# Queries of five row tiles made in natural order at the end of part one; their first 512 rows open part two

## The chip, the cores and the metric

The kernel runs on one core of one Trainium2 chip. Its engines work side by side and each takes its own instructions in order: TensorE (PE in the profile; its weight loads are PEld), VectorE (DVE), ScalarE (ACT), GpSimd (POOL) and SyncE (SP), which issues plain DMAs. GpSimd also issues the indirect DMAs, here called gathers. The metric is the device time of one execution in microseconds; lower is better. The time before is 1229.44 us, the median of three runs (1226.88, 1229.44 and 1234.75).

## The reference

The input x has N = 3327 rows of D = 1024 floats, and adj is a 3327 x 3327 matrix of 0 and 1, symmetric, with ones on the diagonal and few others: a row has from a handful to some tens of neighbours. What is computed is one graph attention layer behind a layer norm:

```python
h = jnp.maximum(_layernorm(x, axis=-1), 0.0)
f = h @ Wf + bf
g = h @ Wg + bg
e = jax.nn.relu(f @ g.T)
scores = jnp.where(adj > 0, e, NEG)
attention = jax.nn.softmax(scores, axis=1)
out = x + attention @ (h @ W + bW)
```

The three weight matrices are 1024 x 1024. A row's softmax runs only over its neighbours.

## The kernel before

The kernel never forms the 3327 x 3327 scores. Since f . g of two rows is h A h with A = Wf Wg^T, it makes A once, then a query q = h A (plus the bias terms) for each row, and takes the dot product of that query with the h row of each neighbour. Rows go in tiles of 128, so there are 26 tiles, the last with 127 rows. A dense path stands behind a flag for inputs with rows of too many neighbours; it does not run here.

**Part one** (some 240 us) goes through the 26 natural tiles. For each it loads the adjacency rows, counts degrees on ScalarE (`degrees`, L697), multiplies the 0/1 row with column numbers on GpSimd (`keys`, L704), takes the largest eight of each of 16 segments on VectorE (`segments`, L767) and builds a list of up to 24 neighbours in `pay` (`listed`). It also loads x, makes layer norm and relu (`measured`, `rooted`, `inverted`, `scaled`), and stores h in DRAM (`hd`). Beside this TensorE transposes Wg and Wf in blocks (`transposed`, `factor`, L821), and makes the products of A in thirds of 342 columns (`product`, L837); a ninth product row holds the bias term `vb`. ScalarE copies each result out of PSUM, in the order in which `empty` finds it. The loop over i issues the degrees and keys of tile i + 2 and the segments and list of tile i. A dictionary `plan` spreads the product steps over the iterations.

A counting sort orders all rows by degree. `one_hot` marks each row's degree among 48 bins; `before` and `after` (L798, L801) accumulate counts in one PSUM tile `pre`; `placed` (L806, the "hit") reads a row's place. At the end 26 small matmuls (L1078) turn places into the order of rows, `perm` (L1092). Part one then gathers the h rows of the first two sorted tiles, transposes them, and makes their q (L1108) on TensorE.

**Part two** (some 970 us) goes through the sorted tiles. The capacity of a tile, `CAPS`, is the largest number of neighbours of its rows; `ORDER` is the sequence in which the tiles are done. For each tile GpSimd gathers the lists (from `pd`), the tile's own h rows (H), and, one gather per neighbour place, 128 h rows (G, all L639). TensorE transposes H and makes q in thirds (L1246). VectorE takes a dot product of each gathered tile with q (L1259, whole result into `junk`, sum into `sc`), masks, and finds the maximum; ScalarE takes the exponentials. The weighted sum of gathered rows is split: `SHARE` says how many rows of a tile's last chunk ScalarE scales and TensorE adds up in PSUM by a transposing matmul (L1295, L1299); VectorE adds the rest (L1312). TensorE then multiplies with W (L1327), and the rows are added to x and scattered to the output.

The order of the instructions of part two is worked out when the program is built: `steps_of` lists all steps with costs and dependences, `planned` runs a list schedule forward and backward 30 times with noise and keeps the best order, and each engine's queue has that order. `FREE_AT` gives the time at which the planner takes each engine as free. The plan only sets orders; what an instruction waits for at run time are its data and buffers. `ROWS` = 26 buffers hold gathered rows; two `junk` tiles take turns.

## Time and profile before

| | us |
|---|---|
| runs | 1226.88, 1229.44, 1234.75 |
| the profiled execution | 1226.98 |
| its span, first to last instruction | 1225.2 |
| VectorE busy | 1116.6 (91%) |
| TensorE busy | 1098.0 (90%) |
| GpSimd busy | 942.2 (77%) |
| ScalarE busy | 602.7 (49%) |

A share of the whole span hides the stages, so the views by stretch of time and the timeline are of more use here. In a line of the timeline the first two numbers are the start and the length in us; then come engine, source line, operation, output and inputs, shapes and count. What stands in brackets at the end is the time for which the engine had been idle, and what ended that.

### The profile page before, as it was taken

Reading aid. Unit: us, or ns where it says so; the run is one execution under the profiler, and the core shown is the slowest. Engines: PE = TensorE matmul, PEld = TensorE weight load, DVE = VectorE, ACT = ScalarE, POOL = GpSimd, SP = SyncE. Lnnn points to the kernel's source line nnn. Section 1 sums busy time; section 2 is a strip of 40 time slices with the busy share of each in tenths; the row PEclk is TensorE's granted clock in tenths of the full one; section 3 lists DMA queues with packets and bytes.
Section 4 is the critical chain, followed back from the end, with each engine's and each line's share of the span. In section 5 each row is a group of like instructions: output and inputs, shape, how many; then the busy total and the mean of one; then the engine's idle time right before and its main releaser. Section 6 shows DMA issues by size and latency. Waiting matters only on the chain. (4 is left out here: it accounts for less than half of the span.)

```text
span 1225.2 us, 14006 instructions
## 1 busy us (share of the span) xinstructions
PE 1098.0 (90%) x4508; PEld 697.0 (57%) x4508; DVE 1116.6 (91%) x2191; ACT 602.7 (49%) x924; POOL 942.2 (77%) x677
## 2 busy tenths in 40 slices
PE   2799990799939899899999999999899999999997
PEld 2566660466628466556665666655465656555553
DVE  5999998659898999999999999898999999999983
ACT  6899887325617355436543365443332434333351
POOL 8999997277677787878888878777787888877841
PEclk9899995799979999999999999999899999999999
DMA  9999999689888999989999998888988989998962
GB/s 369 420 398 396 397 356 338 199 318 339 280 259 278 333 308 316 347 273 326 305 331 316 321 310 299 289 285 296 314 285 284 312 275 320 295 315 258 326 183 54
DMA packets 101913, 374.43 MB, mean 306 GB/s; under 512 B 14859, under 2 KB 18602, under 8 KB 98631
## 3 DMA queue, kind: packets, MB, share of 16 engines
q0 software_dynamic: 79584, 286.77, 69.9%
q1 hardware_dynamic: 22246, 86.68, 18.7%
q8 instruction: 37, 0.61, 0.2%
q14 instruction: 46, 0.38, 0.1%
HBM read 344.11 MB, written 29.30 MB: 305 GB/s over the span
## 5 line engine op out<-in xcount | busy, mean ns | idle before, releaser
L639 POOL DMA_INDIRECT G<-hd,ps x454 | 569.2, 1254 | 152.6 <-issue 96.9
L1259 DVE CUSTOM_DVE_ANT_0 junk<-G,q 128x1024 bf16<-128x1024 f32 x468 | 564.2, 1225 | 35.5 <-DMA G<-hd,ps 21.1
L1327 PE MATMUL p_o<-W_sb,yT 128*128 128x512 f32 x832 | 365.7, 593 | 3.7 <-ACT yT L1323 3.7
L1312 DVE SCALAR_TENSOR_TENSOR G<-G,sc 128x1024 f32<-128x1024 f32 (+1 forms) x281 | 354.8, 1263 | 6.1 <-ACT G L1284 5.4
L1246 PE MATMUL p_q<-A_sb,hT 128*128 128x342 f32 x1152 | 350.3, 455 | 8.7 <-ACT p_q L1255 7.3
L1246 PEld LDWEIGHTS p_q<-A_sb,hT 128*128 128x128 f32 x1152 | 214.4, 191 | 117.0 <-issue 10.0
L1327 PEld LDWEIGHTS p_o<-W_sb,yT 128*128 128x128 f32 x832 | 155.1, 189 | 187.9 <-issue 177.1
L1299 PE MATMUL p_y<-ident,G 128*128 128x128 f32 x1552 | 189.3, 276 | 15.1 <-DVE G L1312 8.3
L1299 PEld LDWEIGHTS p_y<-ident,G 128*128 128x128 f32 x1552 | 174.9, 142 | 43.1 <-ACT G L1295 13.5
L704 POOL TENSOR_TENSOR r<-r,iotaj 128x1664 f32<-128x1664 f32 (+3 forms) x50 | 184.0, 3750 | 3.4 <-ACT r L697 3.4
L1295 ACT ACTIVATE G<-G,sc 128x1024 f32<-128x1024 f32 x168 | 179.1, 1137 | 0.1
L837 PE MATMUL ps_A<-WgT,WfT 128*128 128x342 f32 x432 | 129.7, 458 | 2.4 <-ACT WfT L832 2.4
L767 DVE MAX8 cand<-r 128x8 f32<-128x208 f32 (+2 forms) x416 | 118.9, 360 | 4.2 <-POOL r L704 3.6
L1338 ACT ACTIVATE xp<-p_o,rs 128x512 f32<-128x512 f32 x50 | 34.2, 686 | 174.3 <-PE p_o L1327 131.2
L837 PEld LDWEIGHTS ps_A<-WgT,WfT 128*128 128x128 f32 x432 | 81.3, 192 | 42.3 <-ACT WfT L832 2.5
L697 ACT ACTIVATE r<-r 128x3327 f32<-128x3327 int32 (+3 forms) x27 | 77.3, 2864 | 12.1 <-DMA r<-in_adj_dram 12.1
L1252 ACT COPY q<-p_q 128x342 f32<-128x342 f32 x72 | 31.5, 441 | 103.7 <-PE p_q L1246 74.3
L639 POOL DMA_INDIRECT xp<-in_x_dram,perm x25 | 49.4, 1974 | 19.9 <-ACT xp L1338 13.2
L1280 ACT ACTIVATE sc<-sc,nm 128x10 f32<-128x10 f32 (+10 forms) x36 | 10.9, 303 | 106.2 <-DVE nm L1270 86.6
L1242 ACT COPY hT<-p_t 128x512 f32<-128x512 f32 x48 | 27.3, 585 | 72.3 <-PE p_t L1239 42.9
L1323 ACT COPY yT<-p_y 128x512 f32<-128x512 f32 x52 | 30.0, 586 | 59.9 <-PE p_y L1299 59.9
L1345 POOL DMA_INDIRECT out_dram<-xp,perm x25 | 31.3, 1252 | 35.8 <-DMA xp<-in_x_dram,perm 30.9
(147 smaller groups left out, 724.6 us busy)
## 6 DMA issues: line engine op xcount, KB each, us to landing
r<-in_adj_dram SPq DMA_DIRECT2D x24, 1663.5 KB, 13.1
xt<-in_x_dram SPq DMA_DIRECT2D x22, 512.0 KB, 13.6
hd<-xt SPq DMA_DIRECT2D x22, 512.0 KB, 10.5
G<-hd,ps POOLq DMA_INDIRECT x454, 6.1
A_sb<-in_L_gnn_Wg_dram SPq DMA_DIRECT2D x8, 512.0 KB, 17.1
A_sb<-in_L_gnn_Wf_dram SPq DMA_DIRECT2D x8, 512.0 KB, 12.0
W_sb<-in_L_gnn_W_dram SPq DMA_DIRECT2D x8, 512.0 KB, 6.4
cd<-cand SPq DMA_DIRECT2D x25, 64.0 KB, 12.6
```

Source lines behind the costliest of these rows:

```text
L639: return nc.gpsimd.indirect_dma_start(out=to, out_offset=None, in_=table, in_offset=bass.IndirectOffsetOnAxis(ap=idx, axis=0), **kw,)
L697: nc.scalar.activation(r[:n, b:e], a[:n, b:e], AF.Sign, accum_out=to)
L704: eng.tensor_mul(r[:n, b:e], r[:n, b:e], iotaj[:n, b:e])
L767: nc.vector.max(cands[t][:n, s * 8 : s * 8 + 8], r[:n, s * SW : min(N, (s + 1) * SW)])
L837: nc.tensor.matmul(ps[:, :QB], WfTs[c][:, k, :], WgT[:, k, o : o + QB], start=(k == 0), stop=(k == KD - 1))
L1246: nc.tensor.matmul(ps_q[(3 * t + i) % 2][:, :QB], hT[:, k, :], A_sb[:, k, i * QB : (i + 1) * QB], start=False, stop=(k == KD - 1), skip_gr ...
L1259: nc.vector.tensor_tensor_reduce(junks[k % 2], row(t, k), q[:, :D], 1.0, 0.0, op0=ALU.mult, op1=ALU.add, accum_out=scs[t % 3][:, k : k + 1],)
L1295: nc.scalar.activation(g, g, AF.Copy, scale=scs[t % 3][:, k : k + 1])
L1299: nc.tensor.matmul(ps_y[g][:, c, :], of[:, (4 * g + c) * P : (4 * g + c + 1) * P], ident, is_transpose=True, start=((t, g) not in begun an ...
L1312: nc.vector.scalar_tensor_tensor(y, row_k, scs[t % 3][:, k : k + 1], y, op0=ALU.mult, op1=ALU.add)
L1327: nc.tensor.matmul(ps_o[o], yT[:, k, :], W_sb[:, k, o * CB : (o + 1) * CB], start=False, stop=(k == KD - 1), skip_group_check=True,)
L1338: nc.scalar.activation(to, ps_o[o], AF.Copy, scale=rss[t % 3])
```

## The change

1. At the end of part one the five natural tiles 9, 11, 13, 15 and 17 (`AHEAD`) get their q while their h still lies on the chip: `turn` transposes a tile, `fill` puts the bias into a PSUM bank, `third` multiplies, `stored` copies, and `store_q` writes the tile's q to DRAM (`qd`). These 15 thirds follow the products of A in the same plan (`BEGIN`, `SECOND`, `PERIOD`); the last seven run after the loop, in `go`.
2. Of these 640 rows the 512 of lowest degree among them form the first four tiles of part two (`EARLY`), with capacities 21, 18, 16 and 14, done in the order 14, 16, 18, 21. `several` and `ahead_ranks` rank them among themselves. Their lists are stored on their own (`pd1`, `store_ahead`), and `own` holds their places in `qd` and `pd1`. In part two the H step of these tiles gathers q itself; there is no transposition and no product for them. The other rows are sorted as before into 22 tiles.
3. The sort of the last four natural tiles is done in one go (`pre4`, `less`, `least`) in place of one `before`, `placed`, `after` each.
4. The bias row of the product goes: `bias` multiplies `WgT` with the bias as one column, 9 groups of 8 matmuls, and the result goes through DRAM (`vd`) into `vb`. Wf's first block is loaded earlier, and the three products of the first block are made in iterations 0 to 2.
5. Part one no longer gathers h and makes q for two sorted tiles. W's loads are spread later.
6. G's buffers are one column wider; there is one `junk` tile in place of two, and `masks` and `scs` are narrower.
7. `CAPS`, `ORDER`, `SHARE` and `FREE_AT` are new, and the plan of part two is made anew. The capacities add up to 472 (468 before) and the shares to 184 (168 before).

The core of the diff:

```diff
-CAPS = [37, 25, 23, 22, 21, 21, 20, 20, 19, 19, 18, 18, 17, 17, 17, 16, 16, 15, 15, 15, 14, 14, 13, 13, 12, 11]
-ORDER = [24, 15, *range(15), *range(16, 24), 25]
-SHARE = [9, 11, 18, 12, 10, 9, 10, 8, 7, 7, 8, 8, 5, 8, 4, 4, 4, 4, 3, 3, 3, 2, 3, 0, 5, 3]
+CAPS = [37, 25, 23, 22, 21, 21, 20, 19, 19, 18, 18, 17, 17, 16, 16, 15, 15, 14, 14, 13, 12, 11, 21, 18, 16, 14]
+AHEAD = [9, 11, 13, 15, 17]
+EARLY = len(AHEAD) - 1
+ORDER = [25, 24, 23, 22, *range(22)]
+SHARE = [10, 13, 13, 11, 18, 15, 13, 8, 10, 7, 5, 9, 6, 8, 4, 4, 8, 3, 0, 5, 2, 3, 1, 4, 0, 4]
+BEGIN, SECOND, PERIOD = 40.0, 38.0, 7.5
...
-FREE_AT = {"POOL": 247.6, "PE": 268.5, "ACT": 268.4, "DVE": 246.0, "DMA": 247.0}
+PINS = {("H", EARLY): 0.0, ("H", EARLY + 1): 1.0}
+FREE_AT = {"POOL": 222.0, "PE": 228.0, "ACT": 228.0, "DVE": 237.0, "DMA": 222.0}
...
+        def several(to, ts, start=False):
+            n = len(ts)
+            for j, t in enumerate(ts):
+                count(to[:, j, :], tri, oh[:, t, :], start=start and not j)
+                count(
+                    to[:, j + 1 : n + 1, :], every, oh[:, t, None, :].to_broadcast([P, n - j, NBIN])
+                )
...
+        def bias(c):
+            m = P if c < KD else QW - D
+            for k in range(KD):
+                nc.tensor.matmul(
+                    pv[:m, c : c + 1], WgT[:, k, c * P : c * P + m], bfT[:, k : k + 1], start=(c == k == 0),
+                    stop=(k == KD - 1), skip_group_check=True,
+                )
...
+        def turn(t):
+            hTs[t] = wT.tile([P, KD, P], FP, name="WfT")
+            transposed(hTs[t], xs[t])
+
+        def fill(t, i):
+            banks[t, i] = p_mm.tile([P, CB], FP, name="ps_A")
+            nc.scalar.copy(banks[t, i][:, :QB], vb[:, i * QB : (i + 1) * QB])
+
+        def stored(t, i):
+            nc.scalar.copy(qn[t][:, i * QB : (i + 1) * QB], banks[t, i][:, :QB])
+            if i == 2:
+                q_stores.append(t)
...
+        def store_q():
+            while q_stores:
+                t = q_stores.pop(0)
+                j = AHEAD.index(t)
+                nc.sync.dma_start(qd[j * P : (j + 1) * P, :], qn[t][:, : D + 1])
+
+        def third(t, i):
+            if not i:
+                qn[t] = qpool.tile([P, QW], FP, name="q")
+            for k in range(KD):
+                nc.tensor.matmul(
+                    banks[t, i][:, :QB], hTs[t][:, k, :], A_sb[:, k, i * QB : (i + 1) * QB], start=False, stop=(k == KD - 1),
+                    skip_group_check=True,
+                )
+            emptied1.append(lambda: stored(t, i))
...
+            def turned_g(cs):
+                for c in cs:
+                    if c:
+                        transposed(WgT[:, :, c * P : (c + 1) * P], A_sb[:, c, :D])
+                    empty()
+                    bias(c)
             degrees(0, HALVES)
             keys(0, nc.vector)
+            empty()
+            bias(0)
             degrees(1)
             keys(1, nc.gpsimd)
...
+            turned_g((1, 2))
+            load_w(Wf, 1)
+            load_adj(4)
+            factor(0)
+            empty()
...
             for i in range(NT - 3):
                 degrees(i + 2)
                 keys(i + 2, nc.gpsimd)
...
+                if i < 2:
+                    product(0, i * QB)
+                    turned_g(((3, 4, 5), (6, 7))[i])
+                if i == 1:
+                    biases()
+                    factor(1)
...
-        junks = tiles("junk", 2, [P, D], BF)
+        junk = tiles("junk", 1, [P, D], BF)[0]
...
         def L(t):
-            gather(pis[t % 3], pd[:, :], perm[:, ORDER[t] : ORDER[t] + 1])
+            gather(pis[t % 3], pd1[:, :] if t < EARLY else pd[:, :], near(t))
 
         def H(t):
-            gather(G[buf["H", t]], hd[:, :], perm[:, ORDER[t] : ORDER[t] + 1])
+            to = G[buf["H", t]]
+            gather(to if t < EARLY else to[:, :D], qd[:, :] if t < EARLY else hd[:, :], near(t))
```

After the loop, `go` runs one remaining third at a time: five of them stand in TensorE's queue ahead of the matmuls that find the order of rows, two behind.

369 lines of the change are left out of this document (229 added, 140 removed).

## Prediction

> **What bounds the kernel now.** I read the table of busy time by stretch first, then the timeline where part one hands over to part two, then the timeline of the first 60 us. The columns of the table are the stretch, its length, the busy time of TensorE, of its weight loads, of VectorE, ScalarE and GpSimd (instructions in brackets), the granted clock, the DMA share and GB/s.
>
> ```profile
> span 1225.2 us, 14006 instructions
> ```
> ```profile
> 60.00:80.00 20.00, 20.00 (x80) 13.32 (x80) 19.52 (x81) 19.70 (x31) 20.00 (x7) 1.00 1.03 402
> ```
> ```profile
> 400.00:1000.00 600.00, 570.13 (x2387) 360.60 (x2388) 582.75 (x881) 265.92 (x420) 472.31 (x366) 0.99 0.91 308
> ```
>
> From 60 to 80 us four engines are busy 97% or more, so part one has no idle engine to put work on once it runs. From 400 to 1000 us VectorE is busy 97% and TensorE 95%: part two is paid in VectorE time. The joint between them:
>
> ```profile
> 220.82 0.18 DVE L1092 TENSOR_SCALAR perm<-tens 128x26 int32<-128x26 f32 x1
> ```
> ```profile
> 227.37 1.11 POOL L639 DMA_INDIRECT xt<-hd,perm  x1 [21.33 <-DVE cand L780]
> ...
> 238.72 0.95 POOL L639 DMA_INDIRECT ps<-pd,perm  x1 [8.97 <-DMA pd<-pay]
> ...
> 243.11 0.94 POOL L639 DMA_INDIRECT G<-hd,ps  x1 [0.94 <-DVE mask L1234]
> ```
> ```profile
> 252.56 1.23 DVE L1259 CUSTOM_DVE_ANT_0 junk<-G,q 128x1024 bf16<-128x1024 f32 x1 [9.77 <-ACT q L1128]
> ...
> 266.00 0.15 DVE L1361 CAST flag<-p_y 1x1 int32<-1x1 f32 x1 [5.33 <-PE p_y L1192]
> ```
> ```profile
> 1192.20 10.62 DVE L1312 SCALAR_TENSOR_TENSOR G<-G,sc 128x512 f32<-128x512 f32 x14 [1.02 <-ACT G L1284]
> ```
>
> The order is known at 221.0, the first list gather starts at 238.72, the first row gather at 243.11, the first dot at 252.56 after a wait for q; a second wait of 5.33 follows before tile 1. VectorE then works to 1202.8, and 22.4 us of tail end the span. The last tile has 11 rows of capacity in both orders, so I leave the tail.
>
> **Part two, counted.** Capacities sum to 468 before and 472 after, so four more dots. SHARE sums to 168 and 184, so the weighted additions on VectorE (all rows but row 0 and those of SHARE) fall from 274 to 262.
>
> ```profile
> 253.71 1.22 DVE L1259 CUSTOM_DVE_ANT_0 junk<-G,q 128x1024 bf16<-128x1024 f32 x1
> ...
> 254.86 1.22 DVE L1259 CUSTOM_DVE_ANT_0 junk<-G,q 128x1024 bf16<-128x1024 f32 x1
> ...
> 309.18 1.28 DVE L1312 SCALAR_TENSOR_TENSOR G<-G,sc 128x1024 f32<-128x1024 f32 x1
> 310.38 1.22 DVE L1259 CUSTOM_DVE_ANT_0 junk<-G,q 128x1024 bf16<-128x1024 f32 x1
> ...
> 1188.87 1.22 DVE L1259 CUSTOM_DVE_ANT_0 junk<-G,q 128x1024 bf16<-128x1024 f32 x1
> ```
>
> A dot takes 1.15 (start to start), an addition 1.20: 4 x 1.15 - 12 x 1.20 = -9.8 us. The gap before tile 1 goes, as four tiles no longer need TensorE: -5.3. TensorE loses two tiles of q and gains 16 rows of 8 transposes, a net relief, so VectorE stays the bound.
>
> **One junk tile instead of two.** Consecutive dots now write the same tile. In the trace they overlap: 1.15 apart, 1.22 long, 161 such pairs, of which the first and the last stand above. What a wait inside VectorE costs is seen at the end of part one:
>
> ```profile
> 235.05 0.18 DVE L1150 TENSOR_REDUCE bads<-ne 128x1 f32<-128x26 f32 x1
> ...
> 235.26 0.18 DVE L1151 TENSOR_SCALAR ne<-pay 128x26 f32<-128x26 f32 x1
> ...
> 235.48 0.18 DVE L1152 TENSOR_REDUCE bads<-ne 128x1 f32<-128x26 f32 x1
> 235.58 0.85 DVE L1153 TENSOR_TENSOR r<-r,caps 128x676 bf16<-128x676 bf16 x1
> ```
>
> L1153 shares nothing with L1152 and starts 0.10 after it; L1151 only overwrites what L1150 reads and starts 0.21 after it, 0.03 past its end. A dot held that way would start at 1.22 + 0.03 = 1.25, 0.10 to 0.11 later. Twelve additions fewer and four dots more make some 177 pairs: 19.5 us at most, none if a plain overwrite is not held. Early on gathers rather than VectorE should set the pace, and behind a late row a hold costs nothing, so I take half: +10. The Trainium skill (VectorE: DVE Perf Modes, The DRAIN you can't avoid) has it that the next operation cannot begin until the pipe is empty, so that a semaphore adds nothing; by that the term is 0 and the sum 10 lower. The 0.07 overlap of the dots speaks against it.
>
> **Part one's front.** The change multiplies the bias as 9 groups of 16 small records (bias), puts three products ahead of iteration 3, and takes out the three wide products of the bias row. All sits between the transposes of Wg, and each block's copies on ScalarE stand in its queue ahead of the next degrees (L697), for which GpSimd's key multiply (L704) waits.
>
> ```profile
> 12.85 2.98 ACT L697 ACTIVATE r<-r 128x3327 f32<-128x3327 int32 x1 [3.50 <-DMA r<-in_adj_dram]
> ...
> 35.80 2.98 ACT L697 ACTIVATE r<-r 128x3327 f32<-128x3327 int32 x1
> ```
> ```profile
> 16.00 22.07 POOL L704 TENSOR_TENSOR r<-r,iotaj 128x1664 f32<-128x1664 f32 x6 [2.55 <-ACT r L697]
> 38.94 25.80 POOL L704 TENSOR_TENSOR r<-r,iotaj 128x1664 f32<-128x1664 f32 x7 [0.86 <-ACT r L697]
> ```
> ```profile
> 14.30 1.94 PE L821 MATMUL ps_tr<-ident,A_sb 128*128 128x128 f32 x8 [14.30 <-DMA A_sb<-in_L_gnn_Wg_dram]
> ...
> 45.87 6.77 PE L837 MATMUL ps_A<-WgT,WfT 128*128 128x342 f32 x16 [2.35 <-ACT WfT L832]
> 52.48 1.04 PE L821 MATMUL ps_tr<-ident,A_sb 128*128 128x128 f32 x8
> ...
> 53.41 9.45 PE L837 MATMUL ps_A<-WgT,WfT 128*128 128x342 f32 x32
> ```
> ```profile
> 160.01 0.18 PE L801 MATMUL pre<-oh,low 128*128 128x48 bf16 x1
> 160.04 0.18 PE L798 MATMUL pre<-oh,tri 128*128 128x48 bf16 x1
> ```
> ```profile
> L837 PEld LDWEIGHTS ps_A<-WgT,WfT 128*128 128x128 f32 x432 | 81.3, 192 | 42.3 <-ACT WfT L832 2.5 <-issue 1.4
> L822 ACT COPY WgT<-ps_tr 128x512 f32<-128x512 f32 x16 | 9.1, 585 | 7.2 <-PE ps_tr L821 6.9 <-PE pre L798 0.3
> ```
>
> A record with 128 weight columns and one moving column is not in the trace. Below it stands the bf16 pair, 0.03 apart; beside it the transposes, 1.04 / 8 = 0.13 with 128 columns moving; above it the load's own 0.19. It has the load of the second and the movement of neither, so I take 0.08, 1.3 for 16. By the Trainium skill (TensorE: Matmul & The Clock Gate, LDWEIGHTS) 128 columns take 107 ns; by that, an estimate, 16 take 1.7 and the front slips some 3 us more.
>
> A block is then transposes 1.04 + last copy 0.6 + bias 1.3 = 2.9; a product is 4.7 (9.45 for two). Queue by queue: block 0's copies end at 16.9 (14.30 + 1.94 + 0.6), so the degrees of tile 1 end at 20.0, not 15.9. Copies of blocks 1, 2 and the first Wf block: 26.8; degrees of tile 2: 30.0, where GpSimd's unbroken six records put the keys of tile 2 at 23.4. Product and three blocks end at 40.3 on TensorE, degrees of tile 3 at 42.1 (30.7 before); product, two blocks, one Wf block: 52.7, degrees of tile 4 at 55.8, when GpSimd began tile 4 at 38.94 before: 17 late. The third product ends at 57.4 and the first hit, that of iteration 3, comes at 57.8:
>
> ```profile
> 43.03 0.20 DVE L806 SCALAR_TENSOR_TENSOR hit<-pre,oh 128x48 f32<-128x48 f32 x1
> ...
> 112.93 0.19 DVE L806 SCALAR_TENSOR_TENSOR hit<-pre,oh 128x48 f32<-128x48 f32 x1
> ...
> 198.13 0.19 DVE L806 SCALAR_TENSOR_TENSOR hit<-pre,oh 128x48 f32<-128x48 f32 x1
> ```
>
> That is 15 late. From there VectorE sets 7.8 an iteration ((112.93 - 43.03) / 9) with all four engines full, so nothing wins it back; nine hits fewer (0.27 each) and the 13 small steps of ahead_ranks cancel. The ends of the bias cost make it 9 to 29.
>
> SP's queue is no bound here: the load of Wf 0 now waits for block 0's transposes (16.2) with adjacency 2 behind it, 2.2 MB or 5.4 us at 402 GB/s, ready before 26.8. Later the loads of x 15, 17, 22 and 24 wait for turn to free their tiles, with adjacency loads behind; those turns are due an iteration or more earlier.
>
> **Part one's end.** Iteration 22's hit moves from 198.13 to 213. Seven of the 15 thirds of q, each of a product's shape, are still to come. Nine small matmuls (1.7), five thirds and a turn (5 x 4.7 + 1.0 = 24.5) stand on TensorE ahead of the matmuls that find the order:
>
> ```profile
> 215.54 1.93 PE L1078 MATMUL ps_A<-r 128*128 128x52 bf16 x26 [11.81 <-DVE r L1074]
> ```
> ```profile
> 219.49 2.29 SPq L745 DMA_DIRECT2D hd<-xt  x3
> ```
> ```profile
> 233.49 1.94 PE L821 MATMUL ps_tr<-ident,xt 128*128 128x128 f32 x8 [6.68 <-DMA xt<-hd,perm]
> ```
>
> 213 + 1.7 + 24.5 + 1.9 = 241, seven VectorE steps to own: 242.5, 21 later than perm now. The list gather needs no late list any more, so it starts at once and row gathers at 247 (238.72 to 243.11 is 4.4): 4 late. The last two thirds end at 250.5, their copy at 251; the store of q lands like the last h store (issued by 221.8, free at 227.37: 5.6) at 256.6, the gather of q is usable 6.1 later (227.37 to 233.49), and GpSimd's row gathers queue behind it. First dot: 262.7, +10. ScalarE's 30 extra copies for the thirds stand behind those same matmuls and are within these times. So the late lists and q go, and q's own store and gather take their place. W's loads, which move behind this, land long before the first W product.
>
> **Sum.** +10 - 5.3 - 9.8 + 10 = +5: a span of 1230, and with the 1.8 us around it (1226.98 - 1225.2) 1232 us. The profiled execution lies 2.5 below the median of 1229.44, within the spread of the three runs; I keep 1232.
>
> **Rivals.**
> - *The front hides.* If the bias records run at 0.03 the first dot is at 256; if the copies also slip in between degrees without holding GpSimd, at 252 or, with no slip at all, 248. With free overwrites the sum is -15 to -20: 1207 to 1212. For it: TensorE idles most of the first 45 us, having waited 14.30 for Wg. Against it: GpSimd has one idle stretch of 0.86 in its first 13 records, and the queue order alone puts degrees behind copies. 0.30.
> - *The front is cold, the slower side.* In these 45 us eight transposes take 1.94 and a product 6.77, against 1.04 and 4.7 later. If the gaps between blocks keep TensorE at that pace, bias records are near 0.19, the first hit slips 29 or more and the first dot to 277: 1246, and 1256 with every hold paid. It decides from about 10 us more slip than my 15. 0.23.
> - *Overwrites are free* and the front is as I have it: 1222. 0.12.
>
> **How the numbers follow.** My case, 0.35, is 1232, its own range 1222 to 1242. One per cent, about what a measurement here can tell from no change, is 1217 to 1242. Faster 0.30 (first rival), slower 0.23 (second), the rest 0.47. The range 1204 to 1250 leaves out the coldest front and a gain beyond the first rival.
>
> **What would show it.** In the trace after: GpSimd idle between key multiplies before 60 us and the first hit near 58 (hidden front: 43 to 48); the row of bias records, 0.08 each; perm's step near 242; the first dot near 263, waiting for the gather of q; no gap before tile 1; dots 1.25 apart where no addition lies between. A first dot before 250 or dots still 1.15 apart make the prediction wrong on the fast side.

## The result: 6% slower, and the profile after

The changed kernel takes 1307.27 us (median of 1295.19, 1302.63, 1311.90 and 1322.57), the kernel before 1229.33 in four runs. The ratio is 1.0595, with a 95% interval of 1.05 to 1.069; it leaves out the slowest run, which lies 2.1% above the fastest. I had said 1232, between 1204 and 1250. The profiled execution took 1295.19.

The page of the changed kernel, and then VectorE's timeline of it: the hits of iterations 3, 4, 20 and 21 (L858), the order (L1268), the first dot and two later ones (L1426).

```profile
span 1293.5 us, 14849 instructions
```
```profile
74.41 0.21 DVE L858 SCALAR_TENSOR_TENSOR hit<-pre,oh 128x48 f32<-128x48 f32 x1 [9.06 <-PE pre L821]
...
94.15 0.19 DVE L858 SCALAR_TENSOR_TENSOR hit<-pre,oh 128x48 f32<-128x48 f32 x1
...
216.98 0.19 DVE L858 SCALAR_TENSOR_TENSOR hit<-pre,oh 128x48 f32<-128x48 f32 x1
...
237.14 0.19 DVE L858 SCALAR_TENSOR_TENSOR hit<-pre,oh 128x48 f32<-128x48 f32 x1
...
274.61 0.18 DVE L1268 TENSOR_SCALAR perm<-tens 128x26 int32<-128x26 f32 x1
...
309.56 1.23 DVE L1426 CUSTOM_DVE_ANT_0 junk<-G 128x1024 bf16<-128x1024 f32 x1 [6.60 <-DMA G<-qd,own]
...
316.92 1.22 DVE L1426 CUSTOM_DVE_ANT_0 junk<-G 128x1024 bf16<-128x1024 f32 x1
...
318.19 1.22 DVE L1426 CUSTOM_DVE_ANT_0 junk<-G 128x1024 bf16<-128x1024 f32 x1
```

Against the same steps of before, this says where the time came in:

| step | before | after | later by | new in this stretch |
|---|---|---|---|---|
| first hit (iteration 3) | 43.03 | 74.41 | 31.4 | 31.4 |
| hit of iteration 12 | 112.93 | 155.46 | 42.5 | 11.1, all of it between the hits of iterations 3 and 4 |
| hit of iteration 20 | 175.02 | 216.98 | 42.0 | -0.5 |
| hit of iteration 21 | 183.46 | 237.14 | 53.7 | 11.7 |
| the order (perm) | 220.82 | 274.61 | 53.8 | 0.1 |
| first dot | 252.56 | 309.56 | 57.0 | 3.2 |
| end | 1225.2 | 1293.5 | 68.3 | 11.3 |

Five sixths of the loss lie ahead of the first dot, in three places of part one and a little at the joint. The groups of GpSimd's key multiplies show it from the other side; the number behind the second bar is the time for which GpSimd had stood idle ahead of them. Before, then after:

```profile
L704 POOL TENSOR_TENSOR r<-r,iotaj 128x1664 f32<-128x1664 f32 x24 | 90.1, 3753 | 3.4 <-ACT r L697 3.4
```
```profile
L721 POOL TENSOR_TENSOR r<-r,iotaj 128x1664 f32<-128x1664 f32 x24 | 89.8, 3741 | 55.5 <-ACT r L714 54.7 <-DVE sums L845 0.8
```

The same work, and 51.3 us more of waiting for the degrees that ScalarE counts. All experiments below give their time as a ratio to the kernel before on the same chip. Where I compare times of steps I say with which kernel. The run e13 below is the changed kernel once more, on the chip of e14 to e16. The runs e1 to e4 went on one chip, e5 to e8 on a second, e9 to e12 on a third, e13 to e16 on a fourth, e17 and e18 on a fifth.

### The profile page after: what moved, and what is told of

It reads as the page before. It is cut to its first block, busy times and chain, and to the rows that moved or that the text cites. A ratio compares the mean times of both kernels' runs of the same rounds, so it can differ in the third digit from the quotient of the medians.

```text
span 1293.5 us, 14849 instructions
## 1 busy us (share of the span) xinstructions
PE 1145.8 (89%) x4769; PEld 743.9 (58%) x4769; DVE 1132.5 (88%) x2196; ACT 616.8 (48%) x942; POOL 916.2 (71%) x683
## 5 line engine op out<-in xcount | busy, mean ns | idle before, releaser
L656 POOL DMA_INDIRECT G<-hd,ps x458 | 551.3, 1204 | 188.8 <-issue 102.4
L1426 DVE CUSTOM_DVE_ANT_0 junk<-G,q 128x1024 bf16<-128x1024 f32 x403 | 493.2, 1224 | 20.9 <-DMA G<-hd,ps 14.3
L1479 DVE SCALAR_TENSOR_TENSOR G<-G,sc 128x1024 f32<-128x1024 f32 (+1 forms) x268 | 338.3, 1264 | 4.5 <-ACT G L1451 3.1
L1413 PE MATMUL p_q<-A_sb,hT 128*128 128x342 f32 x1056 | 321.8, 457 | 8.5 <-ACT p_q L1422 3.9
L1413 PEld LDWEIGHTS p_q<-A_sb,hT 128*128 128x128 f32 x1056 | 198.8, 193 | 111.0 <-issue 14.6
L721 POOL TENSOR_TENSOR r<-r,iotaj 128x1664 f32<-128x1664 f32 (+3 forms) x50 | 184.4, 3742 | 55.5 <-ACT r L714 54.7
L1466 PE MATMUL p_y<-ident,G 128*128 128x128 f32 x1680 | 203.6, 277 | 22.6 <-ACT G L1462 12.9
L1466 PEld LDWEIGHTS p_y<-ident,G 128*128 128x128 f32 x1680 | 190.5, 143 | 49.4 <-ACT G L1462 18.1
L1462 ACT ACTIVATE G<-G,sc 128x1024 f32<-128x1024 f32 x184 | 195.9, 1137 | 0.1
L893 PE MATMUL ps_A<-WgT,WfT 128*128 128x342 f32 x384 | 119.3, 470 | 0.0
L1426 DVE CUSTOM_DVE_ANT_0 junk<-G 128x1024 bf16<-128x1024 f32 x69 | 84.5, 1225 | 28.9 <-DMA G<-hd,ps 20.6
L893 PEld LDWEIGHTS ps_A<-WgT,WfT 128*128 128x128 f32 x384 | 74.8, 199 | 37.7 <-issue 4.8
L925 PE MATMUL ps_A<-A_sb,WfT 128*128 128x342 f32 x240 | 73.7, 465 | 0.0
```

Source lines behind the costliest of these rows:

```text
L656: return nc.gpsimd.indirect_dma_start(out=to, out_offset=None, in_=table, in_offset=bass.IndirectOffsetOnAxis(ap=idx, axis=0), **kw,)
L721: eng.tensor_mul(r[:n, b:e], r[:n, b:e], iotaj[:n, b:e])
L893: nc.tensor.matmul(ps[:, :QB], WfTs[c][:, k, :], WgT[:, k, o : o + QB], start=(k == 0), stop=(k == KD - 1))
L925: nc.tensor.matmul(banks[t, i][:, :QB], hTs[t][:, k, :], A_sb[:, k, i * QB : (i + 1) * QB], start=False, stop=(k == KD - 1), skip_group_ch ...
L1413: nc.tensor.matmul(ps_q[(3 * t + i) % 2][:, :QB], hT[:, k, :], A_sb[:, k, i * QB : (i + 1) * QB], start=False, stop=(k == KD - 1), skip_gr ...
L1426: nc.vector.tensor_tensor_reduce(junk, row(t, k), q[:, :D], 1.0, 0.0, op0=ALU.mult, op1=ALU.add, accum_out=scs[t % 3][:, k : k + 1],)
```

## The experiments

### The front: what the bias records do

TensorE's timeline of the changed kernel: the blocks' transposes (L873, eight records), the bias groups (L885, 16 records with one moving column) and the first product (L893).

```profile
14.63 1.94 PE L873 MATMUL ps_tr<-ident,A_sb 128*128 128x128 f32 x8 [14.63 <-DMA A_sb<-in_L_gnn_Wg_dram]
16.40 3.57 PE L885 MATMUL ps_A<-bfT,WgT 128*128 128x1 f32 x16
...
32.02 5.84 PE L893 MATMUL ps_A<-WgT,WfT 128*128 128x342 f32 x16
37.70 1.03 PE L873 MATMUL ps_tr<-ident,A_sb 128*128 128x128 f32 x8
38.97 1.95 PE L885 MATMUL ps_A<-bfT,WgT 128*128 128x1 f32 x16 [0.24 <-ACT WgT L874]
40.78 1.90 PE L873 MATMUL ps_tr<-ident,A_sb 128*128 128x128 f32 x8
```

A bias group takes 3.57 (0.22 a record) at the slow pace and 1.95 (0.12) at the full one, where I had 1.3. And TensorE is slow from 14.63 to 32 us though it has no gap there: transposes take 1.94. A product brings it to full pace (transposes 1.03 at 37.70), one bias group later it is slow again (1.90 at 40.78). Behind the second product the pace holds a little longer: three more bias groups, at 58.76 and 61.88, take 1.95 and 4.04 for two, and the transposes at 65.85 take 1.97. So the bias stream does not only cost its own time, it takes the other work on TensorE to half pace within one to three groups and keeps it there until the next product.

**e4, fillers ahead.** Is it that TensorE came cold to the first transpose, or that the bias records leave it cold?

```diff
+            warm = p_mm.tile([P, CB], FP, name="ps_A")
+            for _ in range(24):
+                nc.tensor.matmul(
+                    warm.rearrange("p (a b) -> p a b", a=2), ident.bitcast(BF)[:, :P],
+                    ident.bitcast(BF)[:, None, :].to_broadcast([P, 2, 2 * P]), start=True, stop=True,
+                )
```

> The changed kernel with 24 filler matmuls of 512 columns ahead of the first transposes, while TensorE has nothing to do (its first work starts at 14.6 us when the first block of Wg has landed). Theory A (TensorE starts slow because it has been idle, and stays fast once it is): transposes 1.03 instead of 1.94 and 16 bias records 1.95 instead of 3.57, the front of 60 us shrinks to some 38 and the first hit comes at 48 to 56 us; time 1268 to 1282. Theory B (one-column matmuls let TensorE become slow again, as at 40.78 and 45.94 us, some 2 to 4 us after a product at full speed): only the first one or two groups run fast, the first hit comes at 70 to 73 and the time is as the changed kernel's.

Measured: 1283.21, ratio 1.0511 [1.0471, 1.0551]; first hit 73.98. The table of busy time by stretch of this run; the column behind the busy times is the granted clock:

```profile
1.50:8.50 7.00, 6.99 (x24) 2.69 (x24) 1.16 (x1) 3.38 (x5) 6.92 (x14) 1.00 0.98 359
8.50:14.40 5.90, 0.05 (x2) 0.01 (x1) 5.76 (x14) 1.05 (x3) 4.46 (x33) 0.78 0.99 320
14.40:31.80 17.40, 17.40 (x80) 16.51 (x80) 9.72 (x39) 7.07 (x9) 7.38 (x2) 0.50 0.91 366
```

The fillers ran from 1.51 to 8.54, and 5.85 us of waiting for Wg made TensorE cold again, so that this run does not test a warm start right up to the transposes. What it shows is the third row: 17.40 us busy out of 17.40, at a granted clock of 0.50, with the same 1.95 and 3.58 for transposes and bias groups as in the changed kernel. There the clock's record seems to begin only with its first change (it reads 1.00 beside those slow transposes), so I take a later stretch of the changed kernel:

```profile
42.50:51.10 8.60, 8.60 (x41) 8.38 (x41) 0.00 (x0) 4.35 (x4) 0.74 (x1) 0.50 0.07 31
```

The Trainium skill (TensorE: Matmul & The Clock Gate, What's actually happening) has the full clock come after some 3.4 us of sustained activity. For the fillers (0.78 in the idle stretch: full at first, then half) and the products the traces agree; for 17.4 us of transposes and one-column records without a break they do not, so being busy in this sense is not enough. The transposes alone are not to blame: in e9 below, which has no bias records, the first 16 take 3.73 from 14.08 on, and the next eight, at 20.14, take 1.15.

**e2, the bias later.** All nine groups go to iterations 4 and 5, the stores of the column to iteration 8, the load of `vb` to 12.

```diff
-                    bias(c)
-            bias(0)
-                bias(KD)
...
+                if i in (4, 5):
+                    for c in range(5 * i - 20, min(KD + 1, 5 * i - 15)):
+                        bias(c)
```

> The changed kernel, but the 72 one-column bias matmuls stand in iterations 4 and 5, behind the products planned there, and no longer between the transposes of the front; their stores go out in iteration 8 and vb is loaded in iteration 12. Theory (the one-column matmuls, 3.57 us for 16 records, and what waits behind them make the front late): they took 26 us of TensorE between 16.4 and 66, so the first hit comes at 46 to 52 us instead of 74.41; SyncE's queue is no longer held, so the later hits are 5 to 12 us behind those of the kernel before instead of 42; the bias takes some 9 us in iterations 4 and 5 and pushes the products there. First dot 272 to 282 instead of 309.6, time 1256 to 1268. Rival (transposes and products at half speed make the front late whatever stands between): first hit at 62 or later, first dot at 297 or later, time over 1280.

Measured: 1281.47, 1.0501 [1.0452, 1.055]. Its TensorE timeline:

```profile
24.21 4.87 PE L893 MATMUL ps_A<-WgT,WfT 128*128 128x342 f32 x16
...
60.69 13.53 PE L885 MATMUL ps_A<-bfT,WgT 128*128 128x1 f32 x80
```

Without bias records the front runs at full pace from the first product on (4.87, where the changed kernel has 5.84), and the first hit comes at 50.06 instead of 74.41. But the records do not get cheap elsewhere: 80 of them take 13.53 (0.17 each) in iteration 4, where VectorE waits for the counts that stand behind them, and the stop of the stores (below) comes as well: hits 74.36 (iteration 5), 89.62 (6), 125.49 (10), 144.42 (11). The gain of 24 at the first hit is down to 3 at the order (271.60).

**e9, no bias at all.** The bias groups, the column's stores and its load go, and `vb` is zero: this kernel leaves out the product of the bias with Wg, and so the bias term of the scores. It prices everything that hangs on it.

```diff
+            nc.gpsimd.memset(vb, 0.0)
...
-                    bias(c)
-            bias(0)
...
-                    biases()
-                if i == 8:
-                    nc.sync.dma_start(vb, vd[None, :].to_broadcast([P, QW]))
```

> The changed kernel without the bias column: its 72 matmuls, the stores and the load of vb are left out, and vb is set to zero, so the biases bf and bg are left out of q. This sizes the fourth item of the change in one run. Theory (the column costs the front 22 us, and 9 to 11 us more where its stores stop the DMA queues): first hit at 50 as with the bias moved to later iterations, no stop behind it, the later hits 7 to 9 us behind those of the kernel before up to iteration 20 (hit at 182 to 184), first dot at 274 to 278 where the changed kernel has 307 to 310, time some 30 us under the changed kernel's 1286. Rival (TensorE's sum of work in part one, with its nine added thirds, sets the end of part one anyway): the hits come that early, but the order's matmuls wait for TensorE's queue, first dot at 285 or later, time within 22 us of the changed kernel's.

Measured: 1266.64, 1.0271 [1.0206, 1.0336]. First hit 49.80, iteration 20 at 178.83 (3.8 later than before, not 42.0), first dot 275.33. The bias and its way through DRAM are worth 34.2 us at the first dot (309.56 - 275.33), or 32.2 against the changed kernel of e7. Of the 31.4 at the first hit 6.8 remain, which I put down to the products and blocks that now stand ahead of iteration 3.

### SyncE's queue: stores of four-byte pieces

SyncE's queue in the changed kernel (start and length of the issue), and DMA in two stretches (its share and GB/s are the last two columns):

```profile
24.60 1.65 SPq L697 DMA_DIRECT2D r<-in_adj_dram  x2
66.15 3.65 SPq L1045 DMA_DIRECT2D vd<-vcol  x8
...
74.37 0.36 SPq L697 DMA_DIRECT2D r<-in_adj_dram  x1
```
```profile
40.00:60.00 20.00, 19.76 (x92) 16.74 (x92) 8.29 (x32) 6.82 (x9) 10.61 (x3) 0.66 0.16 67
60.00:80.00 20.00, 18.99 (x88) 14.03 (x87) 5.33 (x23) 8.91 (x11) 8.52 (x3) 0.74 0.27 16
```

The stores of the bias column stand in SyncE's queue ahead of all later adjacency loads. The queue issues nothing from 26.25 to 66.15, waiting for `vcol`; then nine stores move 1026 values in pieces of four bytes, and the next adjacency load is issued at 74.37, 8.2 us behind the first store. That is two costs in one place: the wait in order, and the stores themselves.

**e1, the stores later** (iteration 8; `vb` loaded in iteration 12):

```diff
-                for k in range(KD):
-                    nc.sync.dma_start(vd[k * P : (k + 1) * P, None], vcol[:, k : k + 1])
...
                 if i == 8:
+                    store_v()
+                if i == 12:
```

> The changed kernel, but the nine small stores of the bias column are issued in iteration 8 and not in iteration 1; vb is loaded in iteration 12 and not 8. Nothing else moves. Theory (SyncE's queue, waiting for the bias column from 24.6 to 66.15 us, held the adjacency loads back): the first hit stays at 74 us, because TensorE's front is the same; the idle times on adjacency data (ScalarE 11.26, VectorE 12.91) go; the second hit comes at 80 to 84 instead of 94.15, the later hits, the first dot and the end 10 to 13 us sooner: first dot near 298, time near 1284 beside 1295 to 1312. Rival (the slow front of TensorE alone sets the shift, the loads would have waited anyway for keys and buffers): the shift at the hits stays at 42 and the time moves by less than 4 us.

Measured: 1289.55, 1.0573 [1.0526, 1.062]. The second hit came at 81.51, 10.0 behind the first (71.56) and not 19.7, as the theory had it. But the 11 us are not won: from iteration 10 to 11 the hits are 22.6 apart (127.66 and 150.26). SyncE's queue and the DMA of this run:

```profile
104.38 14.28 SPq L1051 DMA_DIRECT2D vd<-vcol  x8
118.70 0.34 SPq L1052 DMA_DIRECT2D vd<-vcol  x1
```
```profile
113.00:119.00 6.00, 6.00 (x24) 3.93 (x23) 5.93 (x22) 5.19 (x9) 6.00 (x3) 1.00 0.09 2
```

The column is long ready here; issuing the nine stores alone holds the queue for 14.7 us, and with no load issued behind them all DMA is down to 2 GB/s in the last 6 of these. The stores stop the loads in both places where they were tried.

**e6, stores of whole rows.** TensorE turns the column, so that it leaves in two stores, of rows of 128 values.

```diff
-                for k in range(KD):
-                    nc.sync.dma_start(vd[k * P : (k + 1) * P, None], vcol[:, k : k + 1])
+                nc.tensor.transpose(ps[: KD + 1, 0, :], vcol, ident)
+                nc.scalar.copy(vrow, ps[: KD + 1, 0, :])
+                nc.sync.dma_start(vd[:D].rearrange("(k p) -> k p", p=P), vrow[:KD, :])
```

> The changed kernel, but the bias column (128 x 9) is turned by TensorE into nine rows before it is stored, so that two stores of rows of 512 bytes take the place of nine stores of single floats; place in the order and wait are the same. Theory (beside the wait for the column, the 1026 pieces of 4 bytes themselves stop the DMA queues: in the run with the stores in iteration 8 they held SyncE for 14.28 us and nothing else moved): SyncE goes on to the adjacency loads at 68 to 69 us instead of 74.37, the second hit comes at 85 to 89 us instead of 94.15, first dot and end 6 to 9 us sooner. Rival (only the wait counts, until 66 us): second hit at 93 or later and no more than 2 us in the end.

Measured: 1276.81, 1.0453 [1.0425, 1.0481]. SyncE's queue now goes straight on:

```profile
65.04 0.35 SPq L1049 DMA_DIRECT2D vd<-vrow  x1
...
65.77 0.36 SPq L697 DMA_DIRECT2D r<-in_adj_dram  x1
```

The second hit is at 81.94 against 91.47 in e7, which is the changed kernel on the same chip, iteration 20 at 203.84 against 214.38. So the four-byte pieces cost 10 us. The ranking behind iteration 20 then took 24 us instead of 20 (next part), and 6.8 of the 10.5 were left at the first dot (300.68 against 307.49).

### The ranking: VectorE waits for GpSimd

Between the hits of iterations 20 and 21 lie 20.2 us in the changed kernel, 8.4 before:

```profile
175.02 0.19 DVE L806 SCALAR_TENSOR_TENSOR hit<-pre,oh 128x48 f32<-128x48 f32 x1
...
183.46 0.19 DVE L806 SCALAR_TENSOR_TENSOR hit<-pre,oh 128x48 f32<-128x48 f32 x1
```

`ahead_ranks` runs there. Here are four of VectorE's steps of it in the changed kernel, and GpSimd's key multiplies at the same time:

```profile
218.12 2.00 DVE L844 TENSOR_TENSOR held<-oh,incl 128x240 f32<-128x240 bf16 x1
...
220.80 3.55 DVE L847 TENSOR_SCALAR r<-r 128x5 f32<-128x5 f32 x1
224.38 3.61 DVE L848 TENSOR_SCALAR top<-r 128x5 f32<-128x5 f32 x1
228.02 0.17 DVE L849 TENSOR_SCALAR r<-r 128x5 f32<-128x5 f32 x1
```
```profile
205.07 14.77 POOL L721 TENSOR_TENSOR r<-r,iotaj 128x1664 f32<-128x1664 f32 x4 [0.33 <-ACT r L714]
220.62 7.34 POOL L721 TENSOR_TENSOR r<-r,iotaj 128x1664 f32<-128x1664 f32 x2 [0.78 <-DVE sums L845]
```

L847 and L848 work on five columns and take 3.55 and 3.61; L849, the same kind of step, takes 0.17. The three long ones end at 220.12, 224.35 and 227.99, and GpSimd's multiplies end at 219.84, about 224.3 (half of 7.34) and 227.96: each VectorE step ends within 0.3 us of the multiply beside it. The Trainium skill (SBUF — State Buffer, Who interferes with whom) says that VectorE and GpSimd share a pair of ports, that an operation with two inputs in SBUF needs it against GpSimd's reads, that a step like tensor_scalar can take it too, and that the holder keeps it for the whole instruction. The trace agrees, with 3.6 us for a step of 0.17.

**e5, the small tiles in PSUM.** The tiles that these steps read and write go to spare columns of a PSUM tile, so that no step has two inputs in SBUF.

```diff
+            s0 = pos[:, :NA]
+            r1, top, incl = pos[:, 10:15], pos[:, 16:21], pos[:, 32 : 32 + NBIN]
-            nc.vector.tensor_reduce(sums2[:, 0, :], wide5, AX.X, ALU.add)
+            nc.vector.tensor_reduce(s0, wide5, AX.X, ALU.add)
-            r1 = c1.tile([P, NA], FP, name="r1")
-            top = c1.tile([P, NA], FP, name="top")
```

> The changed kernel, but in the ranking of the 640 rows ahead (thirteen small operations of VectorE in iteration 20) one operand of each operation that had both in SBUF is kept in PSUM, in scratch columns that are free then. Theory (three of them, 2.00, 3.55 and 3.61 us for 240, 5 and 5 columns, ended just when one of GpSimd's multiplications of 3.67 us ended: with both operands in SBUF they wait for GpSimd): each takes 0.2 to 0.5 us, the thirteen take 4 to 5 us instead of 11.9, the step from the hit of iteration 20 to that of iteration 21 falls from 20.2 to 12 to 14 us, the first dot and the end come 7 to 8 us sooner. Rival (the long ones wait for something in their own chain, a result of the operation before): the thirteen take 11 us or more as before, and the end does not move.

Measured: 1282.21, 1.0501 [1.0464, 1.0539]. Two of the three steps in this run, two lines further down:

```profile
215.63 0.41 DVE L846 TENSOR_TENSOR held<-oh,held 128x240 f32<-128x240 bf16 x1
...
216.72 0.17 DVE L849 TENSOR_SCALAR held<-held 128x5 f32<-128x5 f32 x1
```

The stretch fell from 20.2 to 11.9 us: of the 11.7 that it was longer than before, 8.3 were the wait for the port. Of these 8.3 only 2.6 were left at the first dot (304.91 against 307.49 in e7), because the order then waits: from the hit of iteration 22 to the order it took 36.3 instead of 30.3, as the matmuls that find it stand in TensorE's queue behind the thirds of q. That is the queue I had written of, and it takes over as soon as VectorE is earlier.

### The joint: a gather that waits for a check

GpSimd's gathers behind the order in the changed kernel:

```profile
278.42 1.11 POOL L656 DMA_INDIRECT G<-hd,perm  x1 [19.80 <-DMA bWb<-in_L_gnn_bW_dram]
294.84 0.97 POOL L656 DMA_INDIRECT G<-hd,perm  x1 [15.31 <-DVE one L1342]
...
302.79 0.99 POOL L656 DMA_INDIRECT G<-hd,ps  x1 [3.22 <-DMA ps<-pd,own]
```

The second gather's buffer lies over a tile that VectorE's check of the capacities still uses, and that check is VectorE's last step of part one. Every later gather, the lists among them, stands behind it.

**e7, other buffers first.** I renumbered the buffers of the gathered rows.

```diff
+        G = [G[j] for j in [19, 18, 17, 3, 4, 0, 25, ...]]
```

> The changed kernel with the same plan and the 26 row buffers numbered anew, so that the first ones used lie over memory of part one that is free early (the column numbers, the one-hot of the order, x tiles), and those over the work tiles of VectorE's last sixteen us come last. Theory (GpSimd's second gather, into a buffer over the work tile that VectorE frees at 294, held all gathers behind it from 279.8 to 294.84): gathers of lists and q start at 279 to 284, the first dot comes within 3 us of the end of VectorE's list work, at 295 to 299 instead of 309.56, and the end 9 to 14 us sooner. Rival (the gathers wait for stores or for the lists, or dots started sooner only starve, because GpSimd and the DMAs cannot feed them): first dot at 306 or later, or an end that moves by less than 4 us.

Measured: 1285.59, 1.0538 [1.0518, 1.0558]; second gather 292.07, first dot 307.49. Nothing moved, as the second gather still waits for the check; the buffers seem to get their place in the order in which they are first used, not in that of the list. So this run is the changed kernel once more, and served as such above. The edit failed, and the theory was not tested by it.

**e10 and e14, the check early.** The check moves to right behind `own`; e14 is the same kernel beside e13, the changed kernel again, on one chip.

```diff
+            nc.vector.scalar_tensor_tensor(ne, has, 1.0, deg, op0=ALU.max, op1=ALU.is_lt)   # right behind own
+            nc.vector.tensor_reduce(bads[:, 2:3], ne, AX.X, ALU.max)
             ...
-            nc.vector.scalar_tensor_tensor(ne, has, 1.0, deg, op0=ALU.max, op1=ALU.is_lt)   # behind the last lists
-            nc.vector.tensor_reduce(bads[:, 2:3], ne, AX.X, ALU.max)
```

> The changed kernel with the third check of the flag (four operations of VectorE on the work tile, 2.4 us) moved from the end of the list work to right behind own, so that the work tile, over which the second row buffer lies, is free some 16 us sooner. The buffer order run placed its buffers as the changed kernel does (they are placed in the order of first use), so this asks its question again. Theory (GpSimd's second gather waits for that tile until the end of VectorE's list work, 292 in that run, and all gathers queue behind it): second gather at 276 to 281, lists and first rows by 290, first dot 1 to 5 us behind VectorE's list work, at 293 to 297 instead of 307.5, time 9 to 14 us less. Rival (the gathers wait for other things in turn, or part two is paced by its gathers, so that an early dot only starves): first dot at 303 or later, or the time moves by less than 4 us.

> The changed kernel as it is, on the chip of the runs beside it. All theories: first dot 307 to 312, 1.05 to 1.07 of the kernel before. By the theory that gathers pace part two at some 300 GB/s, its part two (first dot to end) is 8 to 14 us longer than that of the kernel before on this chip, for 3.15 MB more of gathers; by the prediction's count it should be 5 us shorter.

> The kernel of the check-early run beside the changed kernel on one chip. Theory (an earlier start of the gathers is an earlier end): first dot 12 to 15 us sooner than the changed kernel's, the end 8 to 14 us sooner. Rival (an early dot only starves: the first tiles' rows come no faster than one in 2.5 us, and the plan's later steps hold it back): the end moves by less than 4 us, and VectorE waits for rows that much longer between the first dot and 600 us.

Measured: e10 1293.05, 1.0512 [1.0432, 1.0591]. Its gathers:

```profile
279.70 0.97 POOL L656 DMA_INDIRECT G<-hd,perm  x1 [0.30 <-issue]
...
285.88 0.94 POOL L656 DMA_INDIRECT G<-hd,ps  x1 [1.45 <-issue]
```

The second gather goes at once, the row gathers 16.9 earlier (302.79 to 285.88), the first dot comes at 294.95 and not 309.56. On one chip e13 took 1320.56 (1.068 [1.0613, 1.0747]) and e14 1301.1 (1.0565 [1.0512, 1.0618]): 1.1% or some 14 us by the ratios, though their intervals overlap a little. That fits the shift of the first dot, 14.6.

### The junk tile: held, and free

**e3.** The kernel before with one `junk` tile in place of two, and nothing else.

```diff
-        junks = tiles("junk", 2, [P, D], BF)
+        junks = tiles("junk", 1, [P, D], BF)
-                junks[k % 2], row(t, k), q[:, :D], ...
+                junks[0], row(t, k), q[:, :D], ...
```

> The kernel before with one junk tile in place of two and nothing else changed. Theory (a dot waits until the one before has written the same tile; pairs start 1.27 us apart in the changed kernel against 1.15 before): some 160 pairs of dots with 0.12 us each are 19 us, and VectorE bounds part two, so 17 to 20 us on the time: 1246 to 1250; the pairs of dots start 1.27 apart, the pairs of dot and addition 1.15 and 1.20 as before. Rival (overwriting the same tile costs nothing, and the longer pairs of the changed kernel come from its wider buffers or from starving): 1229, pairs at 1.15.

Measured: 1219.73, 0.9998 [0.9981, 1.0015]. The dots in this run, and then the waits of VectorE on gathered rows, of this run, of before, and of the changed kernel (total, times, longest):

```profile
249.30 1.22 DVE L1259 CUSTOM_DVE_ANT_0 junk<-G,q 128x1024 bf16<-128x1024 f32 x1
...
250.56 1.22 DVE L1259 CUSTOM_DVE_ANT_0 junk<-G,q 128x1024 bf16<-128x1024 f32 x1
```
```profile
DVE junk L1259 <- DMA G<-hd,ps: 5.1, 5, 1.4
```
```profile
DVE junk L1259 <- DMA G<-hd,ps: 21.1, 22, 3.7
```
```profile
DVE junk L1426 <- DMA G<-hd,ps: 34.9, 31, 7.9
```

The hold is real: dots start some 1.27 apart, as in the changed kernel (316.92 and 318.19), and not 1.15. For 174 pairs that is 21 us of VectorE, and it costs nothing, since 16.0 of them come out of its waits for gathers. So a VectorE that works this much longer does not lengthen part two: it had waited about as long for gathered rows before.

### Part two: GpSimd's issue of gathers

Is it the bytes that set their pace, or the instructions? **e12** is before with one `junk` and 52 more gathers of half rows (13.6 MB); **e15** has 52 more gathers of 100 bytes a row (0.67 MB). **e16** is before itself on the chip of e13 to e15.

```diff
+            if k in (4, 8):
+                gather(sink, hd[:, :].rearrange("n (a d) -> (n a) d", a=2), entry(t, k))   # e12
+                gather(sink, pd[:, :], entry(t, k))                                        # e15
```

> The kernel before with one junk tile (1219.7, the same as with two) and 52 more gathers in part two, two for each sorted tile, of 128 half rows (2 KB each, 13.6 MB in all) into a tile that nobody reads. Theory (part two is paced by its gathers: the DMAs move 302 GB/s there, 89.7 and 89.3% of their time, in the kernel before and in the changed one): 13.6 MB at 302 GB/s are 45 us, so the time rises by 30 to 50, and VectorE waits for rows that much more. By the same rate the changed kernel's six more gathers of rows in part two (four dots and two H) cost 3.1 MB or 10 us, which takes back what its twelve fewer additions save. Rival (VectorE at 97 to 99% busy, or TensorE, paces part two, and the DMAs have a tenth of their time free): the time rises by less than 10 us.

> The kernel before with one junk tile and 52 more gathers in part two at the same places as the half-row ones, each of 128 list rows of 100 bytes into a tile that nobody reads (0.67 MB in all). If the bytes of the gathers pace part two, the time rises by 2 to 10 us; if GpSimd's time to issue a gather paces it (52 times 1.25 us are 65 us), by 30 to 60 like the run with the half rows, which took 51.6.

> The kernel before as it is, for a trace on this chip. First hit at 43 to 44, order at 217 to 221, first dot at 248 to 253, and part two 968 to 973 us long.

Measured: e12 1281.72, 1.0405 [1.032, 1.0491]; e15 1292.21, 1.0502 [1.0433, 1.0572]; e16 1230.81, 1.0001 [0.9957, 1.0045]. A twentieth of the bytes costs no less: 62 us for e15, 51.5 for e12, against a before of 1230.2. My theory of the bytes fell. Here is one of the added gathers of e15 on GpSimd:

```profile
614.92 0.95 POOL L639 DMA_INDIRECT sink<-pd,ps  x1 [0.30 <-issue]
```

A gather holds GpSimd for 0.94 at its shortest, with a gap of 0.30 ahead of it that is not counted as busy: 1.24, and 52 x 1.24 = 64.5. The row of before from 400 to 1000 us has 366 records and 472.31 busy; with 366 x 0.30 that is 582 of 600 us. GpSimd's 79% was 97%, as full as VectorE.

That the 64.5 meets the 62 is in part luck. In e15 VectorE waits 17.8 us at the step that reads the flag of the dense path, in e16 1.9, and that wait hangs on ScalarE and not on gathers (the next table has more of this kind). From 400 to 1000 us of e15 GpSimd with its gaps is at 93% and VectorE at 92%, so neither is full. And both kinds of added gathers bring 128 rows each, so a price by rows in the queues behind GpSimd would look the same. Shown is that the price of a gather does not go by its bytes; that it is GpSimd's time is argued from the row of before.

**e18, another seed of the planner,** in the kernel before (`SEED` 1 to 4; the planned end is 1.3 us later):

> The kernel before with its plan made from another seed; the planned end is 1.3 us later, nothing else changes, part one least of all. If plans of equal planned length run equally long: 1.00 to 1.004 of the kernel before. If the run time depends on the order in ways that the plan's costs do not hold: a difference of 1 to 2% in either direction, and then no more than that can be read into 10 or 20 us of part two between the two kernels.

Measured: 1232.08, 1.0082 [1.0052, 1.0112]. A plan that is 1.3 us longer on paper is 10 us longer on the chip.

So of part two: the changed kernel has six more gathers there, by these figures an estimate of 7.4 us at 1.24, of the 11.3 in the first table. Beside e16 it lost more, 32.9 (1011.9 from the first dot to the end in e13, 979.0 in e16). The sums of busy time over the first 100 us of part two, from 310 in e13 and then from 253 in e16 (DVE is VectorE):

```profile
sum 100.00, PE 66.83 PEld 45.91 DVE 67.08 ACT 37.54 POOL 55.69; mean PE 33.41 PEld 22.96 DVE 33.54 ACT 18.77 POOL 27.84
```
```profile
sum 100.00, PE 91.07 PEld 58.94 DVE 91.80 ACT 43.44 POOL 75.00; mean PE 45.54 PEld 29.47 DVE 45.90 ACT 21.72 POOL 37.50
```

VectorE gets 67.08 us of work done there instead of 91.80, 24.7 less. But that is not the new order of the steps. It is for the most part one wait, shown here by ScalarE's and VectorE's timeline of e13:

```profile
337.78 0.45 ACT L1419 COPY q<-p_q 128x342 f32<-128x342 f32 x1 [21.48 <-remote]
```
```profile
339.90 0.15 DVE L1531 CAST flag<-p_y 1x1 int32<-1x1 f32 x1 [18.71 <-remote]
```

The word remote stands for a wait that ends by something the profile does not show. ScalarE copies a third of q 18 us behind the end of the matmuls in front of it, TensorE and VectorE wait with it, and in the first trace of the same kernel the same copy starts at 319.40 and VectorE does not wait at L1531 at all. In these traces such waits of ScalarE go with the chip more than with the kernel:

| runs | part two, from the first dot to the end | ScalarE's waits of this kind |
|---|---|---|
| e3 (before with one `junk`) | 968.2 | none |
| e1, e2, e4 (changed, same chip) | 970.8 to 975.9 | none |
| e5 to e8 (changed) | 970.8 to 975.7 | none |
| before, changed (the first traces) | 972.6, 983.9 | none, 13.6 |
| e9 to e11 (changed) | 994.9 to 1001.4 | 28.4 to 42.0 |
| e16 (before), e13 (changed) | 979.0, 1011.9 | 31.0, 71.6 |
| e12, e15 (before with more gathers) | 1030.8, 1042.3 | 84.1, 86.7 |

Where none shows, the changed kernel's part two is 3 to 8 us longer than that of e3 beside it, about what six gathers cost. The rest of the losses in part two comes with these waits; what ends them is open.

### The parts together

**e8** keeps the bias and joins four edits: one bias group in each of iterations 4 to 12, row stores, the ranking in PSUM, and e7's renumbering. **e11** is e9 (no bias, so the same part is left out) with the ranking in PSUM and the early check. **e17** is e11 with the plan's start times set to those measured.

```diff
+                if 4 <= i < 5 + KD:      # e8
+                    bias(i - 4)
-FREE_AT = {"POOL": 222.0, "PE": 228.0, "ACT": 228.0, "DVE": 237.0, "DMA": 222.0}     # e17
+FREE_AT = {"POOL": 237.0, "PE": 244.0, "ACT": 244.0, "DVE": 253.0, "DMA": 242.0}
```

> The changed kernel with the bias out of the front (one group of eight one-column matmuls in each of iterations 4 to 12), row stores in iteration 13, the ranking with operands in PSUM, and the new numbers of the buffers. If the four causes add up: first hit 50, no stop at iteration 11, first dot at 270 to 280 instead of 309.6, time 1240 to 1250 where the changed kernel has 1295 to 1312; TensorE, which has three products or nine groups of the bias and nine thirds more than before in part one, then bounds part one, so the kernel before is not reached. If short groups between products run at full speed each takes 1.95 to 2.0 us; if they cool TensorE too, 2.7 to 3.6. Rival (one bound behind all of them, for instance TensorE's sum of work, gives back what each cause frees): first dot at 290 or later, time over 1262.

> No bias column (biases left out as in the run without the bias), ranking with operands in PSUM, and the third check early: all causes named so far taken away. If they add up: 32 us of the bias, 3 to 8 of the ranking, 9 to 14 of the gathers, first dot at 255 to 262 and a time of 1232 to 1242. If TensorE's queue is the bound behind them (24 products, 15 thirds and their transposes from some 40 us on are 200 us, and the order's matmuls stand behind ten thirds of them), the ranking gives nothing and the first dot comes at 266 to 275: 1243 to 1255. The kernel before, 1220 on that chip, is reached in neither case.

> The kernel of the run with all causes taken away (no bias column, ranking in PSUM, check early; biases left out), with the plan of part two made for the times measured there: VectorE free at 253, TensorE and ScalarE at 244, GpSimd at 237 but its bulk of rows from 250 (where buffers come free), in place of 237, 228 and 222. The planned length of part two is the same. Theory (the old plan counts on rows gathered 15 us ahead of the first dot, and its order does not fit when they come 4 to 8 us ahead): part two 10 to 20 us shorter than the 996.5 us of that run, ratio to the kernel before 1.003 to 1.012. Rival (the order is no worse than another, and the longer part two comes from gathers and from dots that hold each other): ratio 1.015 to 1.025 as without the new plan.

Measured: e8 1276.45, 1.0462 [1.0442, 1.0482]. Its first hit is at 49.64, but the rival came true that TensorE's queue takes back what the edits free: a bias group takes only 1.84 between two products, but the counts stand behind both, and VectorE waits for them.

```profile
DVE hit L860 <- PE pre L887: 27.4, 6, 6.3
```

e11: 1254.25, 1.0198 [1.013, 1.0266]. Its first dot starts at 253.45, as early as before (252.56), 56.1 earlier than in the changed kernel. The parts measured one by one come to 54 to 57: 32 to 34 for the bias, 8 for the ranking at its own place (2.6 at the first dot when it was edited alone), 14 to 15 for the check. So all that lies ahead of the first dot is accounted for, and the 2% that are left are part two (996.5 from the first dot to the end). e17: 1239.5, 1.0138 [1.0075, 1.0202], with 966.5 there, but its first dot comes 13.0 later (266.47). It ran on another chip, without the waits of the table, and its interval overlaps e11's, so whether the plan's start times are the cause is open. No version was faster than before.

## Why the prediction was wrong, point by point

- **The front** (my +15 at the first hit, bias records at 0.08). The mechanism, degrees behind copies behind the bias, was right: GpSimd's idle time ahead of the keys went from 3.4 to 55.5. The term was mis-sized: +31.4, with the bias record at 0.22 and 0.12. I had seen slow transposes in the first 45 us and put them down to gaps, in the rival of the cold front, which gave a first hit of 72 or later (74.41 came). But in the changed kernel there are no gaps; transposes with one-column records between them leave the clock at 0.50 (e4). So that rival met the first hit by another cause, which is luck. Without the bias the first hit is 6.8 late (e9).
- **"Nothing wins it back"** held: the shift is 42.5 at iteration 12 and 42.0 at iteration 20.
- **"SP's queue is no bound here"** failed, by 11.1. I followed the loads of weights and x past their waits, and left out the nine stores that the change adds to the same queue, though the list of the change has the way through `vd`. Taken by rows they cost some 10 less (e6).
- **"The 13 small steps of ahead_ranks cancel"** failed, by 11.7. I counted them by their size; three of them waited for GpSimd's port, which was 8.3 of it (e5), and the other steps are the rest.
- **Part one's end** (my order at 241, dot at 262.7). From the hit of iteration 22 to the order I had 28, and 30.4 came (244.18 to 274.61). From the order to the first dot I had 21.7, and 34.95 came: I let the gathers go at once, and one of them waited until 294.84 for VectorE's last check (e10). The row of before that I named as the hit of iteration 22, 198.13, is the first one behind the loop; iteration 22's own is at 191.02. By it the same working gives 206 for that hit and 234 for the order, so the slip hid 7 us of what I missed.
- **One junk tile** (+10, between 0 and 19.5). The hold was there, 1.27 (I had 1.25) and not 1.15; its price in e3 was 0. I had taken half because gathers might set the pace early on; in e3 the waits for them took up 16.0 of the 21.
- **"VectorE stays the bound", -9.8 and -5.3.** The busy shares of 97% and 95% were read rightly, but GpSimd's 79% was not: with the gap ahead of each gather it is 97%, and a gather is not cheap for being small (e15). Part two was to be 15 us shorter but for the junk tile, whose price was 0, and it was 11.3 longer in the first traces. The wait of 5.33 before tile 1 did go, but VectorE waits for gathered rows 34.9 us in place of 21.1 (24.2 in e7, 5.1 in e3).
- **Sum and chances.** I had 0.23 for a slower kernel. That rival had the right place and the right first hit, by the wrong cause, and its 1246 to 1256 held one of the delays; those behind it (11.1 at the stores, 11.7 at the ranking, 3.2 at the joint, 11.3 in part two) add up to more than the front, and the whole lies 57 us above my range.

What stays open: what ends ScalarE's waits in e9 to e16, and so how much of e11's part two (996.5, against 979.0 in e16) and of the prices of e12 and e15 is theirs. Another plan moved before by 0.8% without any other edit (e18), in a trace without such waits, so the order of the steps counts for something, but no run here singles out what in it does. That the 6.8 at the first hit without the bias (e9) are the products and blocks ahead of iteration 3 was not tested. And no run tells which property of the one-column records keeps the clock low.

## What to carry to other kernels

Follow a change through every queue it adds to, the DMA stores too, and price a small instruction by what it shares with its neighbours, not by its size: here nine stores of 4 KB in all, three small steps of VectorE, one check and 72 one-column matmuls cost most of the 57 us that were lost ahead of the first dot. An engine is full when its busy time plus the gaps between its instructions fill the stretch; read the gap in the timeline before you call another engine the bound. A term that can only cost where its engine is the bound is worth testing alone in the kernel before, which takes one edit. And before you put a loss down to the program, compare the same stretch in traces from several chips: the same part two took 971 us on one and 1012 on another.
